# A low-rank expert feed-forward kernel: the last of seven block products made one PSUM bank after the other, the last application in four column steps, x of two of these steps added by a transfer

## The chip, the cores and the metric

The kernel runs on one core of one Trainium2 chip. The metric is the device time of one execution in microseconds (us), lower is better. The engines named below are TensorE (PE, matrix products; PEld is its loading of the stationary operand), VectorE (DVE), ScalarE (ACT), GpSimd (POOL) and SyncE (SP); PSUM is the buffer of eight banks into which PE writes, SBUF the main on-chip memory.

## The reference

For 64 batches, x is 64 x 1024 (rows by hidden columns). What is computed, cut to what matters:

```python
W = weights[condition]                          # one 64 x 64 matrix for each batch
y = einsum('bct,bcd->bdt', x, W)                # rows of a batch mixed by it
logits = y_flat @ gate_w.T + expert_bias        # 4 experts
one_hot = one_hot(argmax(logits))
base_out = einsum('bth,oh->bto', y, W_up)       # 1024 x 1024
z = einsum('nh,erh->ner', y_flat, lora_A)       # rank 8 for each expert
d = einsum('ner,ehr->neh', z, lora_B)           # (scale 1)
out = x + base_out + einsum('neh,ne->nh', d, one_hot)
```

All is float32.

## The kernel before

Two batches make a *pair* of 128 rows, so there are 32 pairs, and two pairs make a group `g` with pairs `a = 2g` and `b = 2g + 1`: 16 groups. The mixing by W and the product with the large weights commute. So the kernel first forms u = x · [gate | lora_A | W_up], which has 1024 + 36 = 1060 columns, and then applies the mixing matrix of each pair to u (*application*).

For groups 2 to 15 the product u of a group is made in 2 x 2 blocks by a Strassen-like scheme of seven block products (`seven`, line 536): left sums S1 to S4 of the halves of x, right sums T1 to T4 of the weights. One block product is 128 rows x 530 columns, with an inner length of 4 x 128 (`k` = 0 to 3). Each fp32 operand is split into a high and a low part, and three matmuls (high·high, high·low, low·high) stand for one. The 530 columns lie in two neighbouring PSUM banks: 264 columns at the end of the first bank, 266 at the start of the second. `product` (line 183) goes through `k`, and for each `k` makes three matmuls into the first bank, then three into the second. Such a two-bank tile is a *chain*; there are three of them. A further two banks, tag `o`, serve the applications.

The order of work is written out by hand. `run` (line 416) goes through the block products in `order`; `at(s, k, fn, ...)` hooks other work behind the `k`-th quarter of product `s` (`k` = -1: ahead of it). All instructions of PE, DVE, ACT and POOL keep this program order on their engine (class `InOrder`); each engine waits in order. SP's transfers are queued in SP's own order.

What is done with u for one pair:

- its columns are rounded to the high part `uh` by ACT, and DVE subtracts to get the low part `ul` (`u_split`, or, apart, `scalar.copy` and `u_low`);
- `apply(i, j)` makes the mixing for a range of columns `COLS[j]` (354, 354, 352) by three matmuls of `uh` and `ul` into an `o` bank (`cond_u`);
- `gate` takes logits and z from the first 36 columns on DVE; `turn` transposes z on PE, ACT copies the result to `zt` and DVE subtracts in its last third;
- `delta` adds the expert's part by one more matmul of these columns; `evict` takes the sum out of PSUM. `finish` is `apply`, `delta`, `evict` in a row.

For pairs 0 to 29 `evict` is an ACT copy into `y`; after the third range POOL issues a transfer that adds x in SBUF (`accum_op`), and SP stores all of `y`. For the last two pairs (a = 30, b = 31, `i >= NP - 2`, line 325) x has been loaded into `y` ahead (`load_y`), DVE adds the PSUM result to it, and SP stores each range by itself.

In the last group (lines 628 to 676) the products come in the order A11·B11, S2·T2, A12·B21, S3·T3, A22·T4, S1·T1, S4·B22. Pair b's first half of u is ready after the fifth product, its second half after S1·T1 (chain `3`: `u_add`, `keep_sum`); pair a's second half needs the last product S4·B22 (chain `5`). During S1·T1 the first range of a is applied and evicted, and b's gate is computed from a chain tile obtained through `wide`/`place`. In the last product (hooks of step 6, lines 656 to 662) come b's sum, its rounding, `turn(b)`, `u_low`, and after `k` = 2 the first two ranges of b. After the product (lines 665 to 676) DVE makes a's second half as two pieces of 178 and 352 columns, ACT rounds them, and the last three ranges follow: b's third, a's second, a's third.

Of the kernel before, what the change touches and what calls it, by code (L numbers as in the profile page):

```python
# [12 lines left out]
ALU = mybir.AluOpType  # L13
# [4 lines left out]
KH = KC // 2  # L18
H = KC * P
E, R = 4, 8  # L20
ER = E * R
G = E + ER
NW = G + H
NB = NW // 2
CUT = 264
LEFT = 512 - CUT
COLS = ((0, 354), (354, 354), (708, 352))
WARM = 24
GATE = (("lg", E), ("mx", 1), ("sc", E), ("m2", 1), ("zm", ER))
HALVES = (slice(0, 64), slice(64, 128))  # L30
# [14 lines left out]
def kernel(  # L45
# [25 lines left out]
    nc = tc.nc  # L71
    NP = x.shape[0]
    NG = NP // 2
    tensor, vector, scalar, pool = (
        InOrder(tc, e) for e in (nc.tensor, nc.vector, nc.scalar, nc.gpsimd)
    )
# [19 lines left out]
    def temp(name):  # L96
        return tp.tile([P, NB], F32, name=name, tag="t")
# [82 lines left out]
    def chain():  # L180
        return psum.tile([P, 1024], F32, name="c", tag="c", bufs=3)

    def product(g, which, hooks):

        for k in range(KH):
            for c, a, b, first in which:
                h, lo = As[g, a]
                for o, n in (
                    (c[:, LEFT:512], slice(0, CUT)),
                    (c[:, 512 : LEFT + NB], slice(CUT, NB)),  # L190
                ):
                    for m, (l, r) in enumerate(((h, wh[b]), (h, wl[b]), (lo, wh[b]))):
                        tensor.matmul(
                            o,
                            l[:, k],
                            r[:, k, n],
                            start=first and k == 0 and m == 0,
                            stop=k == KH - 1 and m == 2,
                            skip_group_check=True,
                        )  # L200
            for kk, fn, *args in hooks:
                if kk == k:
                    fn(*args)

    def body(c):
        return c[:, LEFT : LEFT + NB]
# [7 lines left out]
    def u_low(i, n, src):  # L214
        h, lo = us[i]
        vector.tensor_sub(lo[:, n], src, h[:, n].bitcast(F32))
# [5 lines left out]
    def half(hf):  # L222
        return slice(NB * hf, NB * hf + NB)
# [4 lines left out]
    def u_add(i, c, t):  # L228
        s = ts["u", i] = temp("usum")
        vector.tensor_add(s, body(c), t)  # L230
# [9 lines left out]
    def keep_sum(key, c, t):  # L240
        s = ts[key] = temp("t")
        vector.tensor_add(s, body(c), ts[t])


    def load_y(i):
        ys[i] = yp.tile([P, H], F32, name="y", tag="y")
        nc.sync.dma_start(ys[i], x[i])

    def load_cond(i):
        t = wsel[i] = wsp.tile([P, 64], F32, name="wsel")  # L250
# [11 lines left out]
            scalar.copy(b[p, 0, p], t[p])  # L262
            vector.tensor_sub(b[p, 1, p], t[p], b[p, 0, p].bitcast(F32))

    wide = []

    def place():
        if wide and wide.pop(0):
            return chain()[:, :512]
        return psum.tile([P, 512], F32, name="o", tag="o", bufs=2)  # L270

    def cond_u(o, i, c):
# [2 lines left out]
        for m, (l, r) in enumerate(((b[:, 0], uh), (b[:, 1], uh), (b[:, 0], ul))):  # L275
            tensor.matmul(o, l, r[:, c], start=m == 0, stop=m == 2, skip_group_check=True)

    def apply(i, j):
        c0, n = COLS[j]
        o = os_[i, j] = place()  # L280
        cond_u(o[:, :n], i, slice(c0, c0 + n))

    def ycols(j):
        c0, n = COLS[j]
        s = G if j == 0 else 0
        return slice(s, n), slice(c0 + s - G, c0 + n - G)

# [25 lines left out]
        vector.tensor_sub(zt[p], zp[p, :P], zt[p].bitcast(F32))  # L313

    def delta(i, j):
        s, d = ycols(j)
        tensor.matmul(
            os_[i, j][:, s], zs[i], b3[:, d], start=False, stop=True, skip_group_check=True
        )

    def evict(i, j):

        s, d = ycols(j)
        o = os_.pop((i, j))[:, s]
        if i >= NP - 2:
            vector.tensor_add(ys[i][:, d], o, ys[i][:, d])
            nc.sync.dma_start(out[i, :, d], ys[i][:, d])
            return
        if j == 0:
            ys[i] = yp.tile([P, H], F32, name="y", tag="y")  # L330
        scalar.copy(ys[i][:, d], o)
        if j == 2:
            pool.dma_start(ys[i], x[i], accum_op=ALU.add)
            nc.sync.dma_start(out[i], ys.pop(i))

    def finish(i, j):
        apply(i, j)
        delta(i, j)
        evict(i, j)

# [86 lines left out]
    c = {}  # L427
# [108 lines left out]
    def seven(g):  # L536
# [6 lines left out]
        def at(s, k, fn, *args):  # L543
            h[s].append((k, fn, *args))
# [7 lines left out]
            vector.tensor_add(s[:, r], body(c["4"])[:, r], ts["t7"][:, r])  # L552

        def gate_of_b():
            wide.append(True)
            o = place()
            cond_u(o[:, :G], b, slice(0, G))
            gate(b, o)
            u_split(b, slice(G, NB), ts["last"][:, G:])
# [25 lines left out]
        if not last:  # L585
            order = (
                ("1", "A11", "B11", True),
                ("2", "S2", "T2", True),
                ("3", "S1", "T1", True),
                ("1", "A12", "B21", False),  # L590
                ("2", "S3", "T3", False),
                ("3", "S4", "B22", False),
                ("2", "A22", "T4", False),
            )
            at(0, 2, split_a, g, "S1")
            at(1, 0, split_a, g, "A12")
            at(2, 0, lambda: keep_sum("t6", c["2"], "t1"))
            at(2, 1, split_a, g, "S3")
            at(2, 2, split_cond, a)
            at(3, -1, lambda: keep_sum("t5", c["3"], "t1"))  # L600
            at(3, 2, split_a, g, "S4")
            at(4, -1, lambda: u_of(a, 0, c["1"]))
            at(4, 2, split_a, g, "A22")
            at(5, -1, lambda: u_add(b, c["2"], ts["t5"]))
            at(5, 0, apply, a, 0)
            at(5, 0, gate, a)
            at(5, 0, lambda: u_split(b, half(1), ts["u", b]))
            at(6, 0, turn, a)
            at(6, 0, lambda: u_sum(a, 1, c["3"], ts["t6"]))
            at(6, 2, delta, a, 0)  # L610
            at(6, 2, evict, a, 0)
            at(6, 3, split_cond, b)

            for i in (b + 2, a + 2):
                at(0, 0, load_half, i, 0)
                at(1, 0, load_half, i, 1)
            at(1, 3, load_cond, a + 2)
            at(3, 1, load_cond, b + 2)
            at(2, 3, sums, g + 1, "S1")
            at(3, 3, sums, g + 1, "S2")  # L620
            at(4, 3, sums, g + 1, "S3")
            at(5, 2, split_a, g + 1, "A11")
            at(6, 1, split_a, g + 1, "S2")
            at(6, 3, sums, g + 1, "S4")
            if g == NG - 2:
                for i in (a + 2, b + 2):
                    at(6, 0, load_y, i)
        else:

            order = (  # L630
                ("1", "A11", "B11", True),
                ("2", "S2", "T2", True),
                ("1", "A12", "B21", False),
                ("2", "S3", "T3", False),
                ("4", "A22", "T4", True),
                ("3", "S1", "T1", True),
                ("5", "S4", "B22", True),
            )
            at(0, 2, split_a, g, "A12")
            at(1, 0, split_a, g, "S3")  # L640
            at(2, 0, lambda: keep_sum("t6", c["2"], "t1"))
            at(2, 1, split_a, g, "A22")
            at(2, 2, split_cond, a)
            at(3, -1, lambda: u_of(a, 0, c["1"]))
            at(3, 0, split_a, g, "S1")
            at(3, 1, split_cond, b)
            at(4, -1, lambda: keep_sum("t7", c["2"], "t1"))
            at(4, 0, split_a, g, "S4")
            at(4, 2, apply, a, 0)
            at(4, 2, gate, a)  # L650
            at(5, -1, first_of_b)
            at(5, 0, turn, a)
            at(5, 1, gate_of_b)
            at(5, 2, delta, a, 0)
            at(5, 2, evict, a, 0)
            at(6, -1, lambda: u_add(b, c["3"], ts["t7"]))
            at(6, -1, lambda: scalar.copy(us[b][0][:, half(1)], ts["u", b]))
            at(6, -1, lambda: keep_sum("t8", c["3"], "t6"))
            at(6, 0, turn, b)
            at(6, 0, lambda: u_low(b, half(1), ts["u", b]))  # L660
            for j in (0, 1):
                at(6, 2, finish, b, j)
        run(g, order, h, c)
        cs[g] = dict(c)
        if last:
            wide.extend((True, True, False))
            s = temp("usum")
            pieces = [slice(NB, 708), slice(708, NW)]
            for n in pieces:
                d = slice(n.start - NB, n.stop - NB)  # L670
                vector.tensor_add(s[:, d], body(c["5"])[:, d], ts["t8"][:, d])
                scalar.copy(us[a][0][:, n], s[:, d])
            for n in pieces:
                u_low(a, n, s[:, n.start - NB : n.stop - NB])
            for i, j in ((b, 2), (a, 1), (a, 2)):
                finish(i, j)

    cs = {}
    for g in range(2):
# [47 lines left out]
```

## Time and profile before

| What | Value |
|---|---|
| Median of 3 runs | 421.29 us (420.39 to 421.49) |
| The profiled execution | 420.05 us |
| its span, first to last instruction | 418.3 us |
| granted TensorE clock | 1.000 of full |
| PE busy | 411.3 us, 98% of the span |
| DVE busy | 285.5 us, 68% |
| ACT busy | 186.5 us, 45% |
| POOL busy | 73.7 us, 18% |
| HBM read and written | 43.70 and 16.78 MB, 145 GB/s |

Times in the profile are microseconds from the start of the span, of one execution. Starts of matmuls are exact, their ends are modelled: matmuls are pipelined, so the distance from one start to the next (here called a slot) is what one costs on PE. The profile gives every compute instruction the same source line, 41, that of the wrapper `InOrder`; instructions are told apart by the tiles they write and read: `c` is a chain, `o` an application bank, `uh`/`ul` the two parts of u, `usum` and `t` sums in SBUF, `y` the output rows. `SPq` is SP issuing a transfer. A bracket behind a line gives the idle time of the engine before it and what ended it.

### The profile page before, as it was taken

The page shows a single profiled execution, that of the slowest core. Times are in us where ns is not written, and L with a number is a line of the kernel's source. Part 1 is how long each engine was busy: PE and PEld are TensorE (multiplying, and loading weights), DVE is VectorE, ACT ScalarE, POOL GpSimd, SP SyncE. Part 2 cuts the span into 40 slices and gives each one's busy share as a digit, 9 for nine tenths or more (in the row PEclk, how much of TensorE's full clock was granted, in tenths as well). Part 3 has the DMA queues.
Part 4 walks back from the last instruction along what each step waited for, and adds up shares of the span by engine and source line. Part 5 has one row for each costly group of instructions (what it writes and reads, how often), then busy time and mean ns, then how long its engine had stood idle before and what let it go on. Part 6 is the DMA issues. An engine that isn't in the chain of part 4 may idle for free.

```text
span 418.3 us, 8117 instructions
## 1 busy us (share of the span) xinstructions
PE 411.3 (98%) x3179; PEld 408.4 (98%) x3179; DVE 285.5 (68%) x640; ACT 186.5 (45%) x417; POOL 73.7 (18%) x89
## 2 busy tenths in 40 slices
PE   7999999999999999999999999999999999999995
PEld 7999999999999999999999999999999999999994
DVE  4787775866767666676666767666675776767765
ACT  4757645553434435333453534335343344524521
POOL 2403612021020201102020020202102020020000
PEclk9999999999999999999999999999999999999999
DMA  7969984443655534465443556434465453574334
GB/s 257 346 248 221 242 184 83 115 138 109 177 132 145 116 83 148 130 176 133 98 121 97 170 133 164 116 80 141 118 178 133 119 127 85 156 207 103 94 60 151
DMA packets 25398, 61.00 MB, mean 146 GB/s; under 512 B 3376, under 2 KB 4912, under 8 KB 25360
## 3 DMA queue, kind: packets, MB, share of 16 engines
q1 hardware_dynamic: 18128, 40.99, 27.1%
q0 software_dynamic: 6528, 18.95, 26.5%
q8 instruction: 25, 0.41, 0.4%
q10 hardware_dynamic: 704, 0.54, 0.4%
q14 instruction: 13, 0.11, 0.1%
HBM read 43.70 MB, written 16.78 MB: 145 GB/s over the span
## 4 chain that ended last, share of the span: by engine, by line
PE 91%; DMA 3%; DVE 2%; ACT 1%; POOL 1%; issue 1%; ACTq 0%; DVEq 0%; POOLq 0%
PE c L41 76%; PE o L41 15%; DMA cond_sb<-in_cond_dram 1%; DMA wsel<-in_cw_dram,idx 1%; ACTq L41 0%; DVE ul L41 0%; POOL wsel L41 0%; DVE lB L41 0%; ACT wraw L41 0%; ACT uh L41 0%; POOL bd L41 0%; DVE usum L41 0%; DVE y L41 0%; DVE T L41 0%; POOL bias_sb L41 0%
## 5 line engine op out<-in xcount | busy, mean ns | idle before, releaser
L41 PE MATMUL c<-hT,ah 128*128 128x264 f32 x480 | 140.2, 292 | 0.0
L41 PE MATMUL c<-lT,ah 128*128 128x264 f32 x480 | 137.6, 287 | 0.0
L41 PE MATMUL c<-hT,al 128*128 128x264 f32 x480 | 137.5, 286 | 0.0
L41 PE MATMUL c<-hB,ah 128*128 128x264 f32 (+1 forms) x432 | 125.1, 290 | 1.2 <-ACT hB L41 1.2
L41 PE MATMUL c<-hB,al 128*128 128x264 f32 (+1 forms) x432 | 124.4, 288 | 0.0
L41 PE MATMUL c<-lB,ah 128*128 128x264 f32 (+1 forms) x432 | 124.3, 288 | 0.0
L41 PEld LDWEIGHTS c<-lT,ah 128*128 128x128 f32 x480 | 91.2, 190 | 0.0
L41 PEld LDWEIGHTS c<-hT,al 128*128 128x128 f32 x480 | 91.1, 190 | 0.0
L41 PEld LDWEIGHTS c<-hT,ah 128*128 128x128 f32 x480 | 91.1, 190 | 0.0
L41 PEld LDWEIGHTS c<-hB,ah 128*128 128x128 f32 x432 | 82.6, 191 | 1.5 <-ACT hB L41 1.5
L41 PEld LDWEIGHTS c<-lB,ah 128*128 128x128 f32 x432 | 82.7, 191 | 0.4 <-DVE lB L41 0.4
L41 PEld LDWEIGHTS c<-hB,al 128*128 128x128 f32 x432 | 82.3, 190 | 0.0
L41 POOL DMA_DIRECT2D y<-in_x_dram x30 | 28.4, 948 | 286.3 <-ACT y L41 285.4
L41 ACT COPY y<-o 128x354 f32<-128x354 f32 (+2 forms) x90 | 39.5, 442 | 56.6 <-PE o L41 54.5
L41 ACT CAST uh<-usum 128x530 fp32r<-128x530 f32 (+4 forms) x44 | 27.1, 616 | 72.4 <-DVE usum L41 72.3
L41 DVE TENSOR_TENSOR al<-S,ah 128x512 fp32r<-128x512 f32 x56 | 38.5, 688 | 24.3 <-ACT ah L41 24.3
L41 DVE TENSOR_TENSOR al<-xh,ah 128x512 fp32r<-128x512 f32 x46 | 31.7, 689 | 30.6 <-ACT ah L41 30.6
L41 PE MATMUL o<-uh,bd 128*128 128x354 f32 (+1 forms) x188 | 46.0, 326 | 0.3 <-ACT y L41 0.3
L41 DVE TENSOR_TENSOR ul<-usum,uh 128x530 fp32r<-128x530 f32 (+4 forms) x44 | 30.0, 683 | 18.8 <-ACT uh L41 18.8
L41 ACT CAST zt<-o 96x128 fp32r<-96x128 f32 x32 | 8.4, 261 | 76.3 <-PE o L41 76.2
L41 POOL DMA_INDIRECT wsel<-in_cw_dram,idx x32 | 35.2, 1100 | 9.8 <-issue 5.5
L41 ACT CAST ah<-S 128x512 fp32r<-128x512 f32 x56 | 34.9, 623 | 1.8 <-DVE S L41 1.5
(65 smaller groups left out, 456.7 us busy)
## 6 DMA issues: line engine op xcount, KB each, us to landing
xh<-in_xt_dram SPq DMA_DIRECT2D x60, 256.0 KB, 5.1
y<-in_x_dram POOLq DMA_DIRECT2D x30, 512.0 KB, 5.6
out_dram<-y SPq DMA_DIRECT2D x30, 512.0 KB, 2.8
wraw<-in_w_dram SPq DMA_DIRECT2D x23, 265.0 KB, 5.7
wraw<-in_w_dram POOLq DMA_DIRECT2D x8, 265.0 KB, 6.9
y<-in_x_dram SPq DMA_DIRECT2D x2, 512.0 KB, 4.4
xx<-in_xt_dram SPq DMA_DIRECT2D x1, 512.0 KB, 6.6
wsel<-in_cw_dram,idx POOLq DMA_INDIRECT x32, 5.0
```

Source lines behind the costliest of these rows:

```text
L41: return lambda *a, **k: self.tc.keep_in_program_order(fn(*a, **k))
```

## The change

Four edits, all in the last group, pairs a = 30 and b = 31.

- The last product S4·B22 leaves `order` and is made by a new function that goes through all four `k` for the first bank (264 columns), then through all four for the second (266). Behind the first bank's last quarter come b's first range and the sum and rounding of the first bank's columns; behind the second quarter of the second bank come b's second range and the low part of the first bank's columns. The second bank's columns follow after the product.
- Pair a's columns are applied in the four ranges `LAST`: 354, 176, 264 and 266, where the last two are the columns of the two banks. The second of these no longer needs the last product; it is finished behind S1·T1's last quarter, in the second bank of the chain tile that served b's gate. The last steps are b's third range, then a's third and fourth.
- x of the first two ranges of a (494 output columns) is no longer loaded ahead and added by DVE. ACT copies both ranges out of PSUM, POOL issues an adding transfer of x, and POOL issues their store as well. `load_y` loads the other 530 columns only.
- `turn(b)` and b's sum, rounding and low part stand between S1·T1 and the last product; `turn(b)` comes ahead of b's sum.

```diff
+LAST = ((0, 354), (354, NB - 354), (NB, CUT), (NB + CUT, NB - CUT))
...
+    def banks(c):
+        return (c[:, LEFT:512], slice(0, CUT)), (c[:, 512 : LEFT + NB], slice(CUT, NB))
+
+    def part_of_product(g, c, a, b, first, k, o, n):
+        h, lo = As[g, a]
+        for m, (l, r) in enumerate(((h, wh[b]), (h, wl[b]), (lo, wh[b]))):
+            tensor.matmul(
+                o,
+                l[:, k],
+                r[:, k, n],
+                start=first and k == 0 and m == 0,
+                stop=k == KH - 1 and m == 2,
+                skip_group_check=True,
+            )
...
+    def product_by_bank(g, c, a, b, hooks):
+
+        for m, (o, n) in enumerate(banks(c)):
+            for k in range(KH):
+                part_of_product(g, c, a, b, True, k, o, n)
+                for kk, fn, *args in hooks:
+                    if kk == KH * m + k:
+                        fn(*args)
...
     def load_y(i):
+
         ys[i] = yp.tile([P, H], F32, name="y", tag="y")
-        nc.sync.dma_start(ys[i], x[i])
+        d = slice(FIRST if i == NP - 2 else 0, H)
+        nc.sync.dma_start(ys[i][:, d], x[i][:, d])
...
-    wide = []
+    FIRST = NB - G
 
     def place():
-        if wide and wide.pop(0):
-            return chain()[:, :512]
         return psum.tile([P, 512], F32, name="o", tag="o", bufs=2)
...
-        if i >= NP - 2:
+        if i == NP - 1 or d.start >= FIRST and i == NP - 2:
             vector.tensor_add(ys[i][:, d], o, ys[i][:, d])
             nc.sync.dma_start(out[i, :, d], ys[i][:, d])
             return
-        if j == 0:
+        if i < NP - 2 and j == 0:
             ys[i] = yp.tile([P, H], F32, name="y", tag="y")
         scalar.copy(ys[i][:, d], o)
-        if j == 2:
+        if i == NP - 2 and j == 1:
+            n = slice(0, FIRST)
+            pool.dma_start(ys[i][:, n], x[i][:, n], accum_op=ALU.add)
+            pool.dma_start(out[i, :, n], ys[i][:, n])
+        elif j == 2:
             pool.dma_start(ys[i], x[i], accum_op=ALU.add)
             nc.sync.dma_start(out[i], ys.pop(i))
...
         def gate_of_b():
-            wide.append(True)
-            o = place()
+            ts["w"] = chain()
+            o = ts["w"][:, :512]
...
-                ("5", "S4", "B22", True),
...
-            at(6, -1, lambda: u_add(b, c["3"], ts["t7"]))
-            at(6, -1, lambda: scalar.copy(us[b][0][:, half(1)], ts["u", b]))
-            at(6, -1, lambda: keep_sum("t8", c["3"], "t6"))
-            at(6, 0, turn, b)
-            at(6, 0, lambda: u_low(b, half(1), ts["u", b]))
-            for j in (0, 1):
-                at(6, 2, finish, b, j)
+            at(5, 3, lambda: finish(a, 1, ts["w"][:, 512:]))
         run(g, order, h, c)
         cs[g] = dict(c)
         if last:
-            wide.extend((True, True, False))
-            s = temp("usum")
-            pieces = [slice(NB, 708), slice(708, NW)]
-            for n in pieces:
-                d = slice(n.start - NB, n.stop - NB)
-                vector.tensor_add(s[:, d], body(c["5"])[:, d], ts["t8"][:, d])
-                scalar.copy(us[a][0][:, n], s[:, d])
-            for n in pieces:
-                u_low(a, n, s[:, n.start - NB : n.stop - NB])
-            for i, j in ((b, 2), (a, 1), (a, 2)):
-                finish(i, j)
+
+            turn(b)
+            u_add(b, c["3"], ts["t7"])
+            scalar.copy(us[b][0][:, half(1)], ts["u", b])
+            keep_sum("t8", c["3"], "t6")
+            u_low(b, half(1), ts["u", b])
+            c5, s = chain(), temp("usum")
+
+            def u_bank(m):
+                o, n = banks(c5)[m]
+                vector.tensor_add(s[:, n], o, ts["t8"][:, n])
+                scalar.copy(us[a][0][:, NB + n.start : NB + n.stop], s[:, n])
+
+            def u_bank_low(m):
+                n = banks(c5)[m][1]
+                u_low(a, slice(NB + n.start, NB + n.stop), s[:, n])
+
+            product_by_bank(
+                g,
+                c5,
+                "S4",
+                "B22",
+                [
+                    (3, finish, b, 0),
+                    (3, u_bank, 0),
+                    (5, finish, b, 1),
+                    (5, u_bank_low, 0),
+                ],
+            )
+            w = chain()
+            u_bank(1)
+            u_bank_low(1)
+            finish(b, 2, w[:, :512])
+            finish(a, 2, w[:, 512:])
+            finish(a, 3)
```

More of the change, by code (lines that the diff above doesn't have):

```diff
@@ L186, in product @@
             for c, a, b, first in which:
[L187 to L200, printed above, removed]
+                for o, n in banks(c):
+                    part_of_product(g, c, a, b, first, k, o, n)
             for kk, fn, *args in hooks:
@@ L276, in cond_u, with cols, apply, ycols @@
             tensor.matmul(o, l, r[:, c], start=m == 0, stop=m == 2, skip_group_check=True)
-    def apply(i, j):
-        c0, n = COLS[j]
-        o = os_[i, j] = place()
+    def cols(i, j):
+        return (LAST if i == NP - 2 else COLS)[j]
+    def apply(i, j, o=None):
+        c0, n = cols(i, j)
+        o = os_[i, j] = place() if o is None else o
         cond_u(o[:, :n], i, slice(c0, c0 + n))
-    def ycols(j):
-        c0, n = COLS[j]
+    def ycols(i, j):
+        c0, n = cols(i, j)
         s = G if j == 0 else 0
@@ L315, in delta @@
     def delta(i, j):
-        s, d = ycols(j)
+        s, d = ycols(i, j)
         tensor.matmul(
@@ L321, in evict @@
     def evict(i, j):
-        s, d = ycols(j)
+        s, d = ycols(i, j)
         o = os_.pop((i, j))[:, s]
-        if i >= NP - 2:
+        if i == NP - 1 or d.start >= FIRST and i == NP - 2:
             vector.tensor_add(ys[i][:, d], o, ys[i][:, d])
@@ L328, in evict, with finish @@
             return
-        if j == 0:
+        if i < NP - 2 and j == 0:
             ys[i] = yp.tile([P, H], F32, name="y", tag="y")
         scalar.copy(ys[i][:, d], o)
-        if j == 2:
+        if i == NP - 2 and j == 1:
[3 more added lines that the diff above has]
+        elif j == 2:
             pool.dma_start(ys[i], x[i], accum_op=ALU.add)
             nc.sync.dma_start(out[i], ys.pop(i))
-    def finish(i, j):
-        apply(i, j)
+    def finish(i, j, o=None):
+        apply(i, j, o)
         delta(i, j)
```

## The prediction

> **What bounds the kernel now.** I read the page's engine row first, then the chain of work that ended last, then the timelines of DVE, PE's weight loads, POOL and SP over the last 15 us, and last the transfers there.
>
> ```profile
> PE 411.3 (98%) x3179; PEld 408.4 (98%) x3179; DVE 285.5 (68%) x640; ACT 186.5 (45%) x417; POOL 73.7 (18%) x89
> ```
>
> TensorE is the bound for the whole span. A change at the end can win only PE stalls there, PE work moved into them, and what follows the last matmuls. The chain over the last microseconds (start, length, what) shows how long that is:
>
> ```profile
> 409.38 1.58 PE o L41 x8
> 410.95 0.75 PE c L41 x6
> ...
> 411.73 0.79 DVE usum L41 x2
> ...
> 412.54 0.49 ACT uh L41
> ...
> 413.06 0.53 DVE ul L41
> 413.58 0.87 DVE y L41 x2
> 414.45 0.43 DVEq L721
> ```
>
> The last product's matmuls end near 411.69; then come two DVE adds, an ACT rounding, a DVE subtraction and three DVE adds of x, until 414.87: 3.2 us without a long product. DVE's timeline (start, duration) gives the prices:
>
> ```profile
> 407.31 0.48 DVE L41 TENSOR_TENSOR y<-o,y 128x318 f32<-128x318 f32 x1
> 407.71 0.70 DVE L41 TENSOR_TENSOR usum<-c,t 128x530 f32<-128x530 f32 x1
> 408.32 0.70 DVE L41 TENSOR_TENSOR t<-c,t 128x530 f32<-128x530 f32 x1
> 409.27 0.29 DVE L41 TENSOR_TENSOR zt<-o,zt 32x128 fp32r<-32x128 f32 x1 [0.25 <-ACT zt L41]
> 409.59 0.71 DVE L41 TENSOR_TENSOR ul<-usum,uh 128x530 fp32r<-128x530 f32 x1
> 410.33 0.49 DVE L41 TENSOR_TENSOR y<-o,y 128x318 f32<-128x318 f32 x1
> ```
>
> The next start comes about 0.08 us before an end: spacings of 0.61 us for 530 columns, 0.43 for 352, 0.26 for 178; I read 0.35 for 264. The weight loads show one PE stall inside this stretch, at the second step of pair b, which waits for ul:
>
> ```profile
> 410.36 0.19 PEld L41 LDWEIGHTS o<-ul,bd 128*128 128x128 f32 x1 [0.29 <-DVE ul L41]
> ```
>
> POOL's last adding transfer and SP's last three stores, then the adding transfer's size and time to landing:
>
> ```profile
> 402.07 0.86 POOL L41 DMA_DIRECT2D y<-in_x_dram  x1 [11.15 <-ACT y L41]
> ```
>
> ```profile
> 414.04 1.31 SPq L327 DMA_DIRECT2D out_dram<-y  x3
> ```
>
> ```profile
> y<-in_x_dram POOLq DMA_DIRECT2D x1, 512.0 KB, 5.5
> ```
>
> The last store is issued at 414.95 and takes 2.1 us to land (417.05); 1.25 us later the span ends.
>
> **What the Trainium skill says.** PSUM — Partial Sum Buffer, on bank collisions: two engines must not touch one bank at once, different banks are free. So a sum can be read from one bank while the product fills the other; in the trace every reader of a chain comes after its whole product. VectorE: DVE Perf Modes, "Two Vector instructions with no wait between them": an instruction whose input starts in another quadrant than the last one from that memory is held until the earlier ones finish. The trace agrees: zt reads PSUM from partition 64, and the next PSUM reader (y at 410.33) starts 0.74 us after ul instead of 0.61. DMA: Bandwidth & Descriptors, "SWDGE vs HWDGE vs iDMA": an adding transfer can only be issued from GpSimd, and its anatomy section prices a GpSimd transfer at 2.0 us plus bytes/436 GB/s. That is 3.2 us for 512 KB; the trace shows 5.5, so an adding one is dearer.
>
> **The change part by part.** The "same" starting point is PE's slot 406.89, where S1·T1 ends in both kernels.
>
> Last application of pair a: 354+352 columns become 176+264+266. A 264-column matmul takes a slot of 0.123 us and one of 354 takes 0.163. No 176-column one is shown; a slot of 36 columns takes 0.12 to 0.14, and the skill (TensorE: Matmul & The Clock Gate, LDWEIGHTS) has 128/1.2 = 107 ns for the weights, so it lies between 0.107 and 0.123 and I take 0.123. Twelve slots are 1.48 us where eight were 1.30: +0.18. But four of them (0.49) move ahead of the last product, where they fill PE from 406.89 to 407.38.
>
> PE then: the transposition of b 0.11 (407.63 to 407.86 holds it and one 0.123 slot), to 407.49; bank 0, 12 slots of 0.123, to 408.97; first step of b 0.65, to 409.62; two k of bank 1, 0.74, to 410.36; second step 0.65, to 411.01, whose ul matmul comes at 410.69; two k 0.74, to 411.75, readable at 411.95 (the trace reads about 0.2 after the slot). So the product ends 0.22 later than before (slot 411.53): +0.49 moved in, -0.27 for the stall.
>
> DVE: the add of 318 columns at 407.31 goes (0.40). Its cover was DVE time ahead of the sum; two ACT copies replace it (318 and 176 columns; 354 take 0.45, so 0.44 and about 0.31), ending near 406.8 and 407.9. Behind the second, ACT rounds zt (0.26) to 408.06. The moved transposition now puts zt ahead of b's sum on DVE: zt 408.09, b's sum 408.41 (before 407.71: +0.70), keep_sum 409.02, ACT's rounding of b 409.14 to 409.78, ul 409.81 to 410.52 (before 410.30). PE asks for it at 410.69, so the stall goes with 0.17 to spare. Then, no longer held, b's first add 410.42, bank 0's sum 410.83 (264 columns 0.43, the skill's (N+151)/0.96; 352 measures 0.516 against its 0.524), ACT's rounding 411.29 to 411.69, b's second add 411.25, ul of bank 0 411.72, bank 1's sum 412.07 (0.1 after it could), rounding 412.53 to 412.93, ul 412.96, then the adds 413.31 (352), 413.74 (264), 414.09 (266), end 414.52. The three last spacings are 0.43+0.35+0.43 = 1.21 against 1.29 before. PE's last step waits for ul at 413.39, ends near 413.85, and so is hidden by the adds queued on DVE. Net at DVE's end: 414.52 - 414.87 = -0.35.
>
> Stores: SP has five instead of six from 407.99; the last three carry 441 KB instead of 529 KB, which ran at 529 KB in 1.58 us (414.87 to 416.45). An issue keeps SP about 0.4, so the last comes about 414.65 instead of 414.95; with the smaller last pieces the last bytes are near 416.1: -0.35. The load of x for pair a loses 494 of 1024 columns; it is issued before 374 and lands in 4.4 us, 30 us ahead of its use: nothing.
>
> POOL: behind the copy at 407.9 it issues the adding transfer (0.88), 253 KB. Unknown: half of the measured 3.5 us of moving plus the measured 2.0 around it is 3.75, at most the whole 5.5; I take 4.3, as the 512 KB store of pair 29 (issued 407.99) moves beside it. Lands 412.2; its store, 2.6 by the skill's price, I take 3.0: 415.2. SP's last lands 416.7, so this is hidden by 1.5 us; that is also its price if the cover is gone.
>
> Sum: profiled execution 420.05 - 0.35 = 419.7 (span 417.95, 1.75 around it as now). The median of runs is 1.24 above the profiled one; kept, 421.29 - 0.35 = 420.9.
>
> **Rivals.** (1) The end is bound by PE, not DVE: DVE's spacings are shorter than I read, its last add starts right behind PE's last delta (413.85 to 414.29), the PE slots of 176 columns fall to 0.107, and the three last stores are no longer queued on the engines: -0.58, -0.06 and another -0.3 make about -0.9, 420.4. For it: DVE has 0.1 to 0.4 of slack at several steps. Against: the in-order ACT rounding between bank 1's sum and its ul leaves DVE idle 0.4 us with the add of b behind it. (2) zt ahead of b's sum makes ul late: if ACT's two copies push zt by 0.5 more, PE stalls 0.2 to 0.3 again and everything after moves: about +0.2, 421.5. (3) Slower: POOL's pair lands last. At 5.5 us each from 407.95 it lands 418.95, against 417.05 now: +1.9, 423.2. It decides from a sum of landing times of 8.75 us (416.7 - 407.95); I expect 7.3. (4) The change doesn't do what it says: the wait for a chain is counted for the whole tile, so bank 1's first matmul waits for bank 0's sum (411.26 instead of 409.62): +1.6 on PE, less the forecast's 0.35: +1.3, 422.6. For whole tiles speaks that no PSUM tile here is read in part while written; against it that ACT starts writing columns 36 on of uh at 405.12, while matmuls on its columns 0 to 35 run to 405.2.
>
> **How the numbers follow.** What a measurement of this kernel can tell from no change is 0.3%, 1.26 us. Forecast (-0.35) 0.56; rival 1 0.20; rival 2 0.10; rival 3 0.08; rival 4 0.06. The runs of before spread 420.39 to 421.49, so each case carries about 0.5 either way, and rival 1 has its upper end open, as slots and transfers can each be off by 0.2. Faster by over 0.3%: most of rival 1's better half and the forecast's edge, 0.12 + 0.10 = 0.22. Slower: rivals 3 and 4, and the edge of 2, 0.14. Within: 0.64. The range 419.8 to 422.0 holds the forecast, rival 1 with its spread and rival 2; it leaves out rivals 3 and 4 and a little of rival 1. The forecast's own range is 420.3 to 421.5.
>
> **What would show it.** PE: no wait of a weight load for ul at b's second step, product's end at 411.8 to 412.1 (if 413 or later: rival 4). DVE: zt ahead of the 530-column sum, last add ending 414.3 to 414.7. ACT: two copies to y between 406.3 and 408. POOL: two issues, landing near 412 and 415; landing after 416.7 is rival 3. SP: last issue near 414.65. I am wrong if a wait for an o buffer or for ACT opens a gap on PE after 407.4, or if the median moves by more than 1.3 us.

## The result, and the profile after

The changed kernel is slower: median 423.06 us against 420.76 us, ratio 1.0058 (95% interval 1.0041 to 1.0074), that is 1.7 to 3.1 us.

Single executions differ by several microseconds ahead of the part that was changed, where the two programs are the same. The profiled execution of after is the slowest of its 22 (425.88 us); its PE was busy for 44.84 of the first 50 us, that of before for 47.28, and from there to 400 us PE is busy all the time in both. So the profiles are compared by their *tails*: from one fixed instruction, the transposition of pair a's z in S1·T1, to the end of the span. In PE's timeline (start, length, what) of before and of after that instruction is (the line of the wrapper is 41 before, 42 after):

```profile
404.06 0.29 PE L41 MATMUL o<-ident,z 128*96 128x128 f32 x1
```

```profile
406.64 0.29 PE L42 MATMUL o<-ident,z 128*96 128x128 f32 x1
```

With spans of 418.27 and 424.07 us the tails are 14.20 and 17.43: +3.2 us. (A second profiled execution of before gave 14.21, with the instruction at 404.36. The tail's +3.2 lies just above the interval of the medians; why is not settled. In the changed kernel and every one below that was timed more than once, the median less the tail is 405.6 to 406.9 us, so medians and tails agree within 1.3 us.)

PE's timeline of after shows where the 3.2 us went. The bracket is PE's idle time and what ended it:

```profile
411.96 0.31 PE L42 MATMUL o<-b,zt 96*128 96x318 f32 x1
413.82 0.39 PE L42 MATMUL c<-hB,ah 128*128 128x266 f32 x1 [1.55 <-DVE usum L42]
...
416.55 0.33 PE L42 MATMUL c<-b,zt 96*128 96x352 f32 x1
418.23 0.49 PE L42 MATMUL c<-uh,bd 128*128 128x264 f32 x2 [1.36 <-DVE y L42]
```

PE stands still twice: ahead of the last product's second bank, until DVE has read the first bank, and ahead of a's third range, until DVE has added x to b's third. DVE's timeline has the two readers, and the last add:

```profile
412.32 0.71 DVE L42 TENSOR_TENSOR ul<-usum,uh 128x530 fp32r<-128x530 f32 x1
412.94 0.48 DVE L42 TENSOR_TENSOR y<-o,y 128x318 f32<-128x318 f32 x1
413.34 0.42 DVE L42 TENSOR_TENSOR usum<-c,t 128x264 f32<-128x264 f32 x1
...
417.57 0.52 DVE L42 TENSOR_TENSOR y<-c,y 128x352 f32<-128x352 f32 x1
419.00 0.43 DVE L42 TENSOR_TENSOR y<-c,y 128x264 f32<-128x264 f32 x1 [0.92 <-PE c L42]
419.50 0.43 DVE L42 TENSOR_TENSOR y<-o,y 128x266 f32<-128x266 f32 x1
```

The last add of before was:

```profile
414.36 0.51 DVE L41 TENSOR_TENSOR y<-o,y 128x352 f32<-128x352 f32 x1
```

The sum of the first bank ends at 413.76 and the second bank's first matmul starts at 413.82; the add for b ends at 418.09 and a's matmul starts at 418.23. In both cases reader and writer touch different banks of one two-bank tile. DVE's last add ends 13.30 us into the tail, against 10.82 before: +2.48. The other 0.75 us come behind it: the last store takes longer to land. Its row among the transfers (size, us from issue to landing), after and then before:

```profile
out_dram<-y SPq DMA_DIRECT2D x1, 133.0 KB, 2.8
```

```profile
out_dram<-y SPq DMA_DIRECT2D x1, 176.0 KB, 2.1
```

The chain of work that ended last tells another story:

```profile
410.69 0.87 POOL y L42
411.55 3.52 issue
...
415.10 2.50 DMA out_dram<-y
417.59 0.51 DVE y L42
```

It goes back through POOL's store as if DVE's add at 417.57 had waited for it. But that add starts just ahead of the end of the DVE subtraction in front of it (417.22 to 417.65), as DVE's instructions do when they follow without a wait; the store only happened to land at the same moment. The run without POOL's transfers (below) shows that the chain is wrong here.

### The profile page after: what moved, and what is told of

Same layout as the page of the kernel before. It is cut to its first block, busy times and chain, and to the rows that moved or that the text cites. A ratio compares the mean times of both kernels' runs of the same rounds, so it can differ in the third digit from the quotient of the medians.

```text
span 424.1 us, 8128 instructions
## 1 busy us (share of the span) xinstructions
PE 411.3 (97%) x3183; PEld 408.8 (96%) x3183; DVE 285.0 (67%) x639; ACT 187.0 (44%) x419; POOL 76.4 (18%) x91
## 4 chain that ended last, share of the span: by engine, by line
PE 90%; DMA 5%; issue 1%; DVE 1%; ACT 1%; POOL 0%; ACTq 0%; SPq 0%; POOLq 0%; DVEq 0%
PE c L42 75%; PE o L42 15%; DMA wraw<-in_w_dram 4%; DMA xx<-in_xt_dram 1%; DMA out_dram<-y 1%; DVE ul L42 0%; ACT wraw L42 0%; DVE y L42 0%; POOL y L42 0%; DVE T L42 0%; ACT hT L42 0%; ACT uh L42 0%; ACT ah L42 0%; ACTq L42 0%; ACT y L42 0%
## 5 line engine op out<-in xcount | busy, mean ns | idle before, releaser
L42 PEld LDWEIGHTS c<-hB,ah 128*128 128x128 f32 x432 | 81.6, 189 | 4.0 <-ACT hB L42 2.2
L42 POOL DMA_DIRECT2D y<-in_x_dram x31 | 29.8, 961 | 291.8 <-ACT y L42 286.6
L42 PEld LDWEIGHTS c<-hB,al 128*128 128x128 f32 x432 | 81.4, 189 | 0.0
L42 ACT COPY y<-o 128x318 f32<-128x318 f32 (+2 forms) x91 | 40.1, 442 | 58.2 <-PE o L42 55.8
L42 PE MATMUL o<-uh,bd 128*128 128x354 f32 (+2 forms) x188 | 46.0, 326 | 1.8 <-ACT uh L42 1.5
```

The costliest lines, as they stand in the source:

```text
L42: return lambda *a, **k: self.tc.keep_in_program_order(fn(*a, **k))
```

## The experiments

Lengths are counted from the same transposition. "DVE" is the end of DVE's last add, "stores" the moment when SP has seen all stores land, "drain" the end of POOL's drain (explained below), "tail" the end of the span; each is of one profiled execution. Each ratio is to executions of before that were timed together with the kernel.

| Kernel | DVE | stores | drain | tail | ratio to before (95%) |
|---|---|---|---|---|---|
| before | 10.82 | 13.37 | 6.50 | 14.20 | 1 |
| changed | 13.30 | 16.60 | 15.07 | 17.43 | 1.0058 (1.0041 to 1.0074) |
| c5_split | 11.60 | 14.81 | 15.48 | 16.27 | 1.0058 (1.0035 to 1.0082) |
| w_split | 12.14 | 15.60 | 15.45 | 16.43 | 1.0050 (1.0026 to 1.0075) |
| both_split | 10.42 | 13.77 | 15.29 | 16.07 | 1.0064 (1.0038 to 1.0090) |
| pool_only | 10.53 | 13.09 | 13.92 | 14.70 | 1.0001 (0.9983 to 1.0020) |
| no_pool | 13.37 | 16.55 | 6.53 | 17.38 | 1.0097 (1.0064 to 1.0130) |
| split_no_pool | 10.48 | 13.73 | 6.42 | 14.56 | 1.0017 (0.9999 to 1.0036) |
| split_sp_store | 10.42 | 14.67 | 11.65 | 15.50 | 1.0023 (1.0007 to 1.0038) |
| late_store | 10.82 | 13.88 | 17.65 | 18.43 | 1.0106 (1.0076 to 1.0136) |
| cut_258 | 10.47 | 12.99 | 6.29 | 13.82 | one execution |
| cut_274 | 10.48 | 12.97 | 6.36 | 13.80 | one execution |
| cut_258_reorder | 10.47 | 12.68 | 6.05 | 13.50 | 0.9989 (0.9969 to 1.0009) |

In every row the tail ends 0.8 us after the later of "stores" and "drain". Differences of 1 us are at the edge of what the ratios tell; the tails resolve smaller ones, as the repetition of before at the end of this section suggests.

**The two waits.** Theory: a wait on PSUM is counted for a whole tile. Each of the two places is given two tiles, in both_split together, in c5_split and w_split alone:

```diff
-            c5, s = chain(), temp("usum")
+            c5, s = (chain(), chain()), temp("usum")
...
-                o, n = banks(c5)[m]
+                o, n = banks(c5[m])[m]
...
-            w = chain()
...
-            finish(b, 2, w[:, :512])
-            finish(a, 2, w[:, 512:])
+            finish(b, 2, chain()[:, :512])
+            finish(a, 2, chain()[:, :512])
```

> The changed kernel with separate tiles instead of one two-bank tile in two places: the last product's two banks lie in two chain tiles, and so do the last steps of b and of a. Theory (a wait is counted for a whole tile, not for a bank): both waits of PE in the last 12 us go, the 1.55 us on the first bank's sum and the 1.36 us on b's last add; the time comes to 0.998 to 1.001 of before, 2 to 3 us under the changed kernel, as the forecast's sum had it. Rival (the transfers of POOL or their late landing cost the time): it stays 1 to 2 us above before, ratio 1.003 to 1.005.

> The changed kernel with separate chain tiles for the two banks of the last product only. Theory: the 1.55 us wait at the second bank's first matmul goes, the wait of a's third step for b's last add stays at 1.0 to 1.4 us; DVE's last add is 1.2 to 1.6 us earlier than in the changed kernel, ratio to before about 1.002. Rival (transfers): no more than 0.5 us won.

> The changed kernel with separate chain tiles for the last steps of b and a only. Theory: the 1.55 us wait at the second bank stays, the 1.36 us wait at a's third step goes; DVE's last add is 0.9 to 1.2 us earlier than in the changed kernel (DVE's own queue then sets it), ratio to before about 1.003. Rival (transfers): no more than 0.5 us won.

The waits went as the theory said: c5_split has only the second (1.47 us), w_split only the first (1.56 us), both_split none. The line of c5_split, that of w_split, and the second bank's first matmul in both_split, which follows b's first range without a wait:

```profile
413.86 0.49 PE L42 MATMUL c<-uh,bd 128*128 128x264 f32 x2 [1.47 <-DVE y L42]
```

```profile
414.66 0.39 PE L42 MATMUL c<-hB,ah 128*128 128x266 f32 x1 [1.56 <-DVE usum L42]
```

```profile
411.17 0.29 PE L42 MATMUL c<-hB,ah 128*128 128x266 f32 x1
```

DVE's last add came 1.70, 1.16 and 2.88 us earlier than in the changed kernel. With both gone it ends 0.40 us earlier than before. And yet the tails are only 1.0 to 1.4 us shorter than that of the changed kernel, and the ratios hardly moved. The expected ratio was missed in both_split and in c5_split, while the 1.003 of w_split lies inside its interval. both_split is still 1.6 to 3.8 us slower than before, its tail 1.9 longer; the rival, which blamed the transfers, had 1.003 to 1.005. SP has seen both_split's stores land by 13.77, but the span goes on for 2.3 us. What fills them is in no timeline of the engines, only in the view of the program's last line, where each engine runs the instruction DRAIN and meets the others (count, then shortest, median and longest in ns, first and last start). For both_split:

```profile
L758 POOLq DRAIN  x3: 46/97/6638, 414.4 to 421.5; - x3
L758 SPq DRAIN  x3: 7/7/7, 419.5 to 421.3; - x3
```

and for before:

```profile
L721 POOLq DRAIN  x3: 46/97/8520, 402.0 to 418.0; - x3
L721 SPq DRAIN  x3: 7/7/7, 417.4 to 417.7; - x3
```

POOL's longest DRAIN, here called its drain, begins with the issue of its last transfer: 6.64 us in both_split, from 414.36 to 421.00, while SP was ready at 419.5. Before, POOL's last transfer was issued at 402.07 and a drain of 8.5 us was over by 410.6, unseen.

**POOL's transfers alone.** In the kernel before, x of a's first range (318 columns) is not loaded ahead; ACT copies the range, POOL adds x and stores it:

```diff
+        if i == NP - 2 and j == 0:
+            scalar.copy(ys[i][:, d], o)
+            pool.dma_start(ys[i][:, d], x[i][:, d], accum_op=ALU.add)
+            pool.dma_start(out[i, :, d], ys[i][:, d])
+            return
```

> The kernel before with the transfer part alone: the first range of a (318 columns) is copied by ACT, x is added by a POOL transfer and POOL stores it. Theory: the transfers lie beside PE's work and land before SP's last store; the add of 318 columns leaves DVE; ratio to before 0.998 to 1.001. Rival (transfers cost the time): 1.003 or more, POOL's store landing last.

The ratio is as the theory had it, but neither theory had the drain. POOL's store landed long before SP's last (10.11 against 12.64), so it cost nothing by its landing; DVE ended 0.29 us earlier; but POOL's drain (6.64 us again) ended at 13.92, 0.83 after the stores. The tail is 0.5 us longer, which is too little for the ratio to show.

**The drain by itself.** In the kernel before, the very last store is issued by POOL instead of SP:

```diff
-            nc.sync.dma_start(out[i, :, d], ys[i][:, d])
+            q = pool if (i, j) == (NP - 2, 2) else nc.sync
+            q.dma_start(out[i, :, d], ys[i][:, d])
```

> The kernel before with its last store (pair a, third range) issued by POOL instead of SP: the disputed cost by itself. Theory of the drain: POOL issues 10.9 us into the tail, drains for 6.6 us, and 0.7 us of barrier follow: tail 18.1 to 18.4 us, +4 us on before, ratio about 1.009. Rival (only the landing counts): the store lands 2.6 to 2.9 us after its issue instead of 2.1, tail 14.7 to 15.0, ratio 1.001 to 1.002.

The drain's theory held, in tail (18.43, where 18.1 to 18.4 were expected) and ratio. The store landed after 2.17 us, at 13.29, and the span waited 5 us more. POOL's timeline, then the view of the last line:

```profile
415.09 0.58 POOL L41 DMA_DIRECT2D out_dram<-y  x1 [12.25 <-DVE y L41]
```

```profile
L722 POOLq DRAIN  x3: 46/97/6557, 415.1 to 422.1; - x3
```

**With and without, both ways.** The transfer part is undone (`load_y` loads all of x, `evict` adds with DVE and SP stores, for pair a's first two ranges too), once with separate tiles and once without:

```diff
-        d = slice(FIRST if i == NP - 2 else 0, H)
+        d = slice(0, H)
...
-        if i == NP - 1 or d.start >= FIRST and i == NP - 2:
+        if i >= NP - 2:
```

> Separate tiles in both places, and the transfer part undone: x of pair a is loaded whole, DVE adds it to the first two ranges and SP stores them. Tail lengths are counted from the start of the transposition of pair a's z in S1·T1 to the end of the span: 14.2 us before, 17.4 changed, 16.1 with separate tiles alone. Theory (after its last transfer POOL sits 6.64 us in a drain at the program's end, and with the PE waits gone this sets the end): without POOL's late transfers the tail is 14.0 to 14.5 us; ratio to before 0.998 to 1.002. Rival (it is SP's stores that land late): the tail stays above 15.5.

> The changed kernel with the transfer part undone, the two-bank tiles as they are. Theory: PE's two waits set the end of the changed kernel and POOL's drain ended 1.5 us earlier there, so the tail stays at 17.0 to 17.5 us, ratio about 1.006. Rival (POOL's transfers are a cost in the changed kernel too): 1 us or more is won.

With the waits in place POOL's transfers cost nothing in the tail: no_pool's is 17.38 against 17.43. Its ratio, from six executions, lies above the expected 1.006, and its interval only just meets that of the changed kernel; the tail does not show why. Its DVE ends at 13.37, though there is no late POOL store that DVE could have waited for: the chain's reading falls. With the waits gone they cost 1.5 us: 16.07 against 14.56. So the drain hides behind the waits, and once the waits are gone it keeps about half of what they cost: without the transfers alone the tail is 0.05 us shorter, without the waits alone 1.4, without both 2.9. The 14.56 is just above the expected 14.0 to 14.5, and 0.36 above before though DVE ends 0.34 earlier. The last store is late: 2.67 us to landing.

**POOL adds, SP stores.** One line more in both_split:

```diff
-            pool.dma_start(out[i, :, n], ys[i][:, n])
+            nc.sync.dma_start(out[i, :, n], ys[i][:, n])
```

> Separate tiles in both places; POOL still adds x to pair a's first two ranges, but SP stores them. Theory of the drain: POOL's last transfer is issued 4.0 us into the tail, its drain (8.5 us behind an adding transfer in the kernel before) ends by 12.7, ahead of SP's last landing near 13.3: tail 14.0 to 14.6 us, ratio 0.998 to 1.002. Rival (landing of the pair): as with POOL's store, 15.5 or more, or SP's stores wait for the adding transfer and end later than 15.

The drain was out of the way (11.65), but the tail was 0.9 us above what the theory allowed, in the manner named last under the rival. SP's waits show it: the store of a's first two ranges stands at the head of SP's queue and waits there for the adding transfer,

```profile
SPq L352 <- DMA y<-in_x_dram: 4.4, 1, 4.4
```

and five more stores, two of them ready earlier, leave behind it within 2.4 us. The last one takes 3.16 us to land. This run also shows what the drain depends on. POOL's last transfer is an adding one here, as before, and its drain is 7.63 us where before has 8.52:

```profile
L758 POOLq DRAIN  x3: 46/97/7629, 408.4 to 419.6; - x3
```

The 247 KB of this run land 4.61 us after their issue, the 512 KB of before after 5.54. In both the drain ends 3.0 us behind the landing.

**The late last store.** In the changed kernel a's last range begins at output column 758, byte 3032 of a row. Two other cuts of the last product put that at a multiple of 64 bytes (3008 and 3072), in split_no_pool (the first bank's columns then stand at the start of their tile):

```diff
-LAST = ((0, 354), (354, NB - 354), (NB, CUT), (NB + CUT, NB - CUT))
+CUT5 = 258
+LAST = ((0, 354), (354, NB - 354), (NB, CUT5), (NB + CUT5, NB - CUT5))
```

> The kernel with separate tiles and no late POOL transfers (tail 14.56 us, its last store of 1064-byte rows from byte 3032 landing 2.67 us after issue) with the cut at 258 alone. Theory (rows of a store that begin at a multiple of 64 bytes land sooner): 2.1 us to landing, tail 13.9 to 14.1. Rival (a third store close behind two others lands late whatever its rows): 2.6 to 2.8, tail 14.5.

> The same with the cut at 274: last range of a from output column 768, rows of 1024 bytes from byte 3072. Theory of the start at a multiple of 64 bytes: 2.0 to 2.1 us to landing. Rival: 2.6 to 2.8.

In both the last store landed sooner, after 1.93 and 1.91 us. The transfers of split_no_pool, then of cut_258 (the last store is the 133 KB one, then the 136 KB one):

```profile
out_dram<-y SPq DMA_DIRECT2D x1, 133.0 KB, 2.7
out_dram<-y SPq DMA_DIRECT2D x1, 132.0 KB, 2.1
```

```profile
out_dram<-y SPq DMA_DIRECT2D x1, 136.0 KB, 1.9
out_dram<-y SPq DMA_DIRECT2D x1, 129.0 KB, 1.9
```

The tail fell by 0.74 us to 13.82, just what the last store gained (1.93 us to landing where it took 2.67); 2.1 had been expected. Why is left open: the old boundary both starts the last store off a 64-byte step and lies inside a 64-byte step shared with the store about 0.5 us ahead of it. The 129 KB store of cut_258 starts off the step as well (byte 1976) and takes 1.9, which speaks for the second. No run separates the two.

**A version with a shorter tail than before.** cut_258 with b's third range ahead of the low part:

```diff
             u_bank(1)
-            u_bank_low(1)
             finish(b, 2, chain()[:, :512])
+            u_bank_low(1)
```

> Separate tiles, no late POOL transfers, the last product cut at 258 columns instead of 264 (last range of a: output columns 752 to 1023, rows of 1088 bytes starting at byte 3008, a multiple of 64), and b's third range ahead of the low part of the second bank's columns, so that DVE adds x for b while ACT rounds. Theory: DVE's last add comes 0.2 to 0.5 us earlier than with the old order, the last store lands 2.1 us after its issue: tail 13.5 to 13.9 us against 14.2 before, ratio 0.997 to 1.001. Rival (the order gains nothing, the store stays late): tail 14.4 or more.

The tail is 13.50, 0.7 us shorter than before. The gain was not where it was expected: DVE's last add ends at 10.47 in both orders, since it now waits for PE (0.28 us); b's store leaves 0.7 us earlier and the last store lands 1.86 us after issue. The ratio, 0.9989, does not tell the kernel from before. The kernel before once more:

> The kernel before once more, to see how far the tail of one profiled execution can be trusted: all theories expect 14.2 us, within 0.15.

It gave 14.21, its last add at 10.82 and its last store at 13.00, 0.01 us from the first time. It is the only kernel that was profiled twice; the other tails are of one execution each.

## Why the prediction was wrong

The forecast was 420.9 us with a range of 419.8 to 422.0; measured were 423.06. It was counted from 421.29 for the kernel before, whose larger set of executions has 420.76, so as a change -0.35 us was forecast and +2.3 measured.

**Slots, DVE's sum.** Right, as both_split shows, the change without its two waits. From the transposition, zt was forecast at 4.03 and came at 3.94, b's sum at 4.35 and 4.26, the last add's end at 10.46 and 10.42. The stall for ul in b's second step went. The product ended 0.16 later for 0.22. The 176-column steps took 0.42 us for 0.49: 0.105 a slot, just under the lower end (0.107) of the forecast's bracket, of which it took the upper. DVE's add of 264 columns took 0.42 us for 0.43; this price is the Trainium skill's (VectorE: DVE Perf Modes, "The TRN2 errata — SBUF-src ops pay a fixed extra latency per instruction"). The reading that a slot of 36 columns takes 0.12 to 0.14 was wrong: the line with the 0.14 holds two matmuls.

**The waits (rival 4).** This is the step that failed. On PE the forecast lets the second bank follow b's first step at 409.62 without a wait ("two k of bank 1, 0.74, to 410.36"), and it lets a's third step start without a wait for b's add. Measured were waits of 1.55 and 1.36 us at these two places. The sign that it named for rival 4, the product's end at 413 or later, came: the changed kernel has it 9.43 us into the tail, 413.5 on the forecast's scale.

Yet rival 4 had the smallest chance of all, 0.06. Its "against" does not carry that: ACT writing columns of uh in SBUF while PE reads others was taken as evidence for PSUM tiles, and those 0.1 us of overlap rest on matmul ends, which are modelled. The forecast itself had noted that no PSUM tile of the kernel before is read in part while written, which left the question open. And it looked at one place, the last product; the tile of b's and a's last steps is shared in the same way. The price of the first was near (forecast 1.6 on PE, measured 1.55); the second's 1.36 was left out. At DVE's end the two are worth 2.88 us, where 1.6 was priced.

That a bank may be read while another is filled, as the Trainium skill has it (PSUM — Partial Sum Buffer, "PSUM bank collisions raise a hardware error"), agrees with both_split, where DVE reads the first bank from 412.40 to 412.82 and PE goes on filling the second, in another tile, at 412.57. But it says nothing of whether the program lets it: in the changed kernel the bank was free, the wait was on the tile.

**POOL (rival 3).** The landings were right: the adding transfer was forecast to land 8.1 into the tail and POOL's store at 11.1; they came at 8.17 and 11.01. "Hidden by 1.5 us" was wrong as a statement of its cover, since what has to be covered is not the landing but the drain, which ends 4.1 us later and stands nowhere in the sum. In the changed kernel it stays hidden all the same, as PE's waits push the end back; in the kernel that the forecast meant, it costs 1.5 us.

**Stores.** "With the smaller last pieces the last bytes are near 416.1: -0.35" failed. The sum took the size alone; the 133 KB store took 2.83 us to land, where the forecast's 414.65 and 416.7 leave about 2.1: +0.73 against before.

Together, in the tail: -0.40 (sum on DVE) +2.88 (two waits) +0.75 (behind DVE's last add, nearly all of it the last store) = +3.23, which is the measured difference split up by both_split. The drain adds nothing to it.

## What to carry to other kernels

Before a forecast builds on two engines working in two banks of one tile, find a place in the profile where a tile in PSUM is read in part while the rest is written; where there is none, give each bank a tile of its own. A transfer from POOL is finished for the program not when it lands but when POOL's drain is over, so in kernels like this one the last one belongs about 7 to 9 us ahead of the end (drains of 6.6 to 8.6 us and the 0.8 us behind them). When a repair removes a wait and the time stays, look at the program's last line, to see which engine comes last to the final meeting.

## What the runs showed of the hardware

- POOL's drain at the end of a program starts with the issue of its last transfer. Behind a plain store it lasted 6.56 to 6.64 us in six kernels, whatever the size (159 to 247 KB) and although the store landed after 2.2 to 2.8 us. Behind an adding transfer it followed the landing: it ended 2.95 to 2.99 us behind it in eight profiles, and so lasted 8.1 to 8.6 us for 512 KB and 7.63 for 247 KB. The span ended 0.8 us behind the later of this drain and SP's last wait. Why the drain is so long, and whether the kind of transfer or the time of its landing decides between the two cases, no run shows. The last line's view alone shows it.
- An adding transfer of 247 KB took 4.1 to 4.6 us to land in five kernels, a plain store of the same size from POOL 2.5 to 2.8 us in four.
- The last store, of 128 rows, took 2.67 to 2.83 us to land in six kernels where its row began at byte 3032, about 0.5 us behind the store that ended there (and 3.16 in a seventh, where the stores were crowded), and 1.86 to 1.93 in three where the boundary was at byte 3008 or 3072.
